# Four graph layers on one core: the last layer's attention rebuilt on stacked hi and lo fp32r pairs, shifts from norms, sums over 63 coordinates

## The chip, the cores and the metric

The kernel runs on one core of one Trainium2 chip. The metric is the device time of one execution in microseconds (us), smaller being better. A run is of state "fast" when it lies within 1.5% of the fastest of its kernel; a kernel that was run only once has state "unknown" and is called a single look here.

## The reference, cut to what matters

Eight batches of 2048 nodes with 64 features pass four graph layers over one adjacency matrix; each is followed by a residual layer norm. The change touches the last one:

```python
def _gat_layer(h, mask, b):
    scores = jnp.einsum('...nd,...md->...nm', h, h)
    scores = jnp.where(mask, scores, NEG)
    attn = jax.nn.softmax(scores, axis=-1)
    return jnp.einsum('...nm,...md->...nd', attn, h) + b
# B, N, C, H, D = 8, 2048, 64, 4, 64
mask = graph + jnp.eye(N, dtype=graph.dtype) > 0
h = jnp.einsum('bnc,hdc->bhnd', x, Wh)                     # four heads
out_h = _gat_layer(h, mask[None, None], bh[None, :, None, :])
cat = jnp.transpose(out_h, (0, 2, 1, 3)).reshape(B, N, H * D)
z = jax.nn.leaky_relu(cat, negative_slope=0.2)
h2 = jnp.einsum('bnk,dk->bnd', z, Wo)
out2 = _gat_layer(h2, mask[None], bo)                      # the "fifth" attention
z2 = jax.nn.leaky_relu(out2, negative_slope=0.2)
# then a layer norm with gamma and beta, + x, and a layer norm without
```

So there are 8 x 5 = 40 attentions, each with a 2048 x 2048 matrix of scores. All is fp32, and the scores go through an exponential, so they need nearly full fp32 accuracy. The input x of the layer is already layer-normed: its 64 features sum to zero, so 63 of them determine the last.

## The kernel before

One attention in layer 3 has two parts. `prepare` makes the projections and finds each row's maximum, in bf16, with a matrix product and a mask product for each tile of 128 x 512 scores. `attend` computes the scores again in fp32, transposed (source node on the partitions), takes the exponential and multiplies the weights by [h | 1].

```python
# prepare: the row maxima
for it in range(NT):                       # NT = 16 tiles of 128 rows
    for c in range(NCH):                   # NCH = 4 chunks of 512 columns
        pa = ps_a.tile([P, CW], F32, name="pa")
        nc.tensor.matmul(pa, hb[:, it * P:(it + 1) * P], hb[:, cs], start=True, stop=False)
        nc.tensor.matmul(pa, neg_id_bf, M[:, it, cs], start=False, stop=True)
        nc.vector.tensor_reduce(mx[:, it, c:c + 1], pa, AX.X, ALU.max)
# ... minus the maxima become the 65th row of the moving side hm ...

# attend: scores, weights, sums
for jt in range(NT):
    pscore = ps_s.tile([P, CW], F32, name="pscore")
    nc.tensor.matmul(pscore, neg_id_bf, MT[:, jt, cs], start=True, stop=False)
    nc.tensor.matmul(pscore, hs[:, jt * P:(jt + 1) * P], hm[:, cs], start=False, stop=True)
    w = wk.tile([P, CW], F32, name="w", bufs=3)
    nc.scalar.activation(w, pscore, AF.Exp)
    nc.tensor.matmul(po, hones[:, jt, hp, hk:hk + 2, :]..., w, start=(jt == 0), stop=(jt == NT - 1))
# ... reciprocal of the denominators, product, bias, leaky relu, product with Wo ...
```

The mask is a matrix product too: minus 2^100 times the identity, times a 0/1 tile in fp8, added into the same accumulator.

## Time and profile before

| | before |
|---|---|
| time, median of the first three runs | 9961.56 us (9957.68 to 9962.04) |
| TensorE / VectorE / ScalarE / GpSimd busy | 92% / 42% / 19% / 6% |
| layers 0 to 2 end at | about 2050 us |
| layer 3, first score to last sum | 2162 to 9932 us |
| granted TensorE clock, mean | 0.914 |

The list of waits over layer 3 adds who waits for whom. Its columns are the waiting engine and line, the engine and line that released it, the total, the number of waits and the longest:

```profile
...
ACT w L564 <- PE pscore L562: 5867.9, 2560, 75.9
DVE rec L567 <- PE po L565: 2836.9, 159, 30.3
...
DVE mx L542 <- PE pa L541: 1192.1, 1502, 4.8
PEld po L565 <- ACT w L564: 1161.0, 1897, 1.6
```

ScalarE and VectorE wait for TensorE, 5868 us at the exponential alone. The last line is the other way round, a weight load of TensorE that is held for the exponential. Most of this passes beside running products.

```profile
6008.02 0.30 PEld L565 LDWEIGHTS po<-w,hones 128*128 128x128 f32 x2 [0.71 <-ACT w L564]
```

The second of two sums starts only when this load does. Two fp32 sums take 1.871 us from start to start in the median of such stretches of this trace (6008.98 - 6007.11 in the prediction's timeline), and 1.715 in the run fp32_sums below, where nothing holds them. So about 0.155 us per two tiles of 512, or 1280 x 0.155 = 199 us in all, goes into this wait (an estimate from the starts). The idle time of 2.1 us that the page gives ahead of the sums (the group L565 in the prediction) does not show it, as the ends of matmul records are modelled. Apart from that the layer hangs on TensorE.

### The profile page before, as it was taken

What the parts mean: (1) busy time and instruction counts of PE and PEld (TensorE: products, weight loads), DVE (VectorE), ACT (ScalarE), POOL (GpSimd) and SP (SyncE); (2) the same over time, 40 slices, a digit from 0 to 9 for tenths busy, and PEclk for the clock granted to TensorE, in tenths of its full rate; (3) what the DMA queues carried; (4) which work ended last, traced back from release to release, by engine and by line L of the source; (5) the groups of instructions that cost most, each with busy time, mean ns of one, the idle gap of its engine ahead of it and who ended that gap; (6) DMA issues with size and microseconds to landing.
All of it is one profiled execution on the core that took longest, in us unless ns stands there. A gap on an engine that the chain in (4) does not pass through costs nothing. (4 is left out here: it accounts for less than half of the span.)

```text
span 9967.4 us, 62454 instructions
## 1 busy us (share of the span) xinstructions
PE 9215.5 (92%) x24992; PEld 3477.5 (35%) x24992; DVE 4228.1 (42%) x5463; ACT 1870.1 (19%) x3156; POOL 597.4 (6%) x471
## 2 busy tenths in 40 slices
PE   3786698679999999999999999999999999999998
PEld 2332244223333333333333333333333333333332
DVE  6899423454334333433443343334333433243423
ACT  1000200012212221222122212221222122212221
POOL 4100301310000000000000000000000000000000
PEclk6898799869989998999899989997999899989997
DMA  2000000000000000000000000000000000000000
GB/s 86 0 0 1 0 0 1 0 1 0 0 0 3 0 0 0 3 0 0 0 3 0 0 0 3 0 0 0 2 0 0 0 3 0 0 0 3 0 0 2
DMA packets 43381, 29.87 MB, mean 3 GB/s; under 512 B 40977, under 2 KB 41041, under 8 KB 41041
## 3 DMA queue, kind: packets, MB, share of 16 engines
q1 hardware_dynamic: 26448, 21.68, 0.7%
q10 hardware_dynamic: 16640, 4.20, 0.2%
q8 instruction: 195, 3.19, 0.1%
q14 instruction: 98, 0.79, 0.0%
HBM read 21.68 MB, written 4.19 MB: 3 GB/s over the span
## 5 line engine op out<-in xcount | busy, mean ns | idle before, releaser
L565 PE MATMUL po<-w,hones 128*128 128x512 f32 x5120 | 2656.5, 622 | 2.1 <-ACT w L564 2.1
L562 PE MATMUL pscore<-hm,hs 65*128 65x512 f32 x5120 | 2650.8, 598 | 0.0
L564 ACT ACTIVATE w<-pscore 128x512 f32<-128x512 f32 x2560 | 1528.6, 597 | 5867.9 <-PE pscore L562 5867.9
L542 DVE TENSOR_REDUCE mx<-pa 128x1 f32<-128x512 f32 x2560 | 1720.9, 691 | 1220.2 <-PE pa L541 1219.2
L567 DVE RECIPROCAL rec<-po 64x512 f32<-64x512 f32 x160 | 536.6, 3353 | 2864.2 <-PE po L565 2864.2
L565 PEld LDWEIGHTS po<-w,hones 128*128 128x128 f32 x5120 | 880.2, 191 | 1245.8 <-ACT w L564 1161.0
L562 PEld LDWEIGHTS pscore<-hm,hs 65*128 65x128 f32 x5120 | 984.7, 193 | 758.1 <-issue 630.7
L540 PE MATMUL pa<-hb 64*128 64x512 bf16 x2560 | 1119.5, 437 | 33.7 <-DVE hb L533 17.2
L541 PE MATMUL pa<-M,neg_id_bf 128*128 128x512 fp8e4 x2560 | 1126.7, 440 | 0.0
L561 PE MATMUL pscore<-MT,neg_id_bf 128*128 128x512 fp8e4 x2560 | 974.8, 382 | 0.2 <-ACT M L458 0.2
L540 PEld LDWEIGHTS <-hb 64*128 64x128 bf16 x2560 | 242.4, 95 | 1299.2 <-issue 1281.3
L270 PE MATMUL acc<-w,H 128*128 128x512 f32 x1024 | 489.1, 632 | 54.0 <-DVE w L267 53.2
L541 PEld LDWEIGHTS <-neg_id_bf 128*128 128x128 bf16 x2560 | 249.6, 97 | 738.6 <-issue 738.6
L534 POOL COPY hm<-hs 64x512 f32<-64x512 f32 x160 | 110.3, 691 | 6234.9 <-ACT hs L532 6234.9
L368 PE MATMUL pa<-R,A 128*128 128x512 f32 x1024 | 453.4, 599 | 9.7 <-POOL R L359 9.3
L561 PEld LDWEIGHTS <-neg_id_bf 128*128 128x128 bf16 x2560 | 249.1, 97 | 474.3 <-issue 469.1
L270 PEld LDWEIGHTS acc<-w,H 128*128 128x128 f32 x1024 | 198.7, 201 | 339.3 <-issue 204.3
L267 DVE SCALAR_TENSOR_TENSOR w<-MT,w 128x1024 f32<-128x1024 fp8e4 x256 | 302.1, 1215 | 0.4
L160 POOL TENSOR_TENSOR ln_rstd<-ln_var,mhalf 128x16 f32<-128x16 f32 (+1 forms) x21 | 151.0, 7189 | 2450.2 <-DVE ln_var L157 2450.2
L368 PEld LDWEIGHTS pa<-R,A 128*128 128x128 f32 x1024 | 191.3, 190 | 269.1 <-issue 245.9
L416 PE MATMUL pa<-Y,A 128*128 128x512 f32 x512 | 219.9, 592 | 0.0
L549 DVE COPY hm<-pm 1x512 f32<-1x512 f32 x160 | 109.0, 682 | 248.4 <-PE pm L548 248.4
(184 smaller groups left out, 3891.9 us busy)
## 6 DMA issues: line engine op xcount, KB each, us to landing
at<-in_adj SPq DMA_DIRECT2D x16, 1024.0 KB, 5.2
X<-in_x ACTq DMA_DIRECT2D x16, 256.0 KB, 7.8
out<-O SPq DMA_DIRECT2D x8, 512.0 KB, 3.8
wt<-in_L_gnn_Wh SPq DMA_DIRECT2D x4, 32.0 KB, 4.6
wo<-in_L_gnn_Wo SPq DMA_DIRECT2D x1, 64.0 KB, 6.0
a<-in_L_gnn_a SPq DMA_DIRECT2D x2, 32.0 KB, 2.9
g<-in_L_gnn_ln_gamma SPq DMA_DIRECT2D x2, 32.0 KB, 2.9
b<-in_L_gnn_ln_beta SPq DMA_DIRECT2D x2, 32.0 KB, 3.1
```

What stands on the lines that cost most here:

```text
L267: nc.vector.scalar_tensor_tensor(w, MT[:, jt, ih * HW:(ih + 1) * HW], 0.0, w, op0=ALU.is_equal, op1=ALU.mult)
L270: nc.tensor.matmul(acc[c], H[:, jt, p, k:k + 2, :].rearrange("p a d -> p (a d)"), w[:, c * CW:(c + 1) * CW], start=(jt == 0), stop=False)
L368: nc.tensor.matmul(pof, A[:, jt], R[:, jt, h].rearrange("p a f -> p (a f)"), start=(jt == 0), stop=False)
L416: nc.tensor.matmul(po, A[:, jt], Y[:, jt], start=(jt == 0), stop=(jt == NT - 1))
L540: nc.tensor.matmul(pa, hb[:, it * P:(it + 1) * P], hb[:, cs], start=True, stop=False)
L541: nc.tensor.matmul(pa, neg_id_bf, M[:, it, cs], start=False, stop=True)
L542: nc.vector.tensor_reduce(mx[:, it, c:c + 1], pa, AX.X, ALU.max)
L561: nc.tensor.matmul(pscore, neg_id_bf, MT[:, jt, cs], start=True, stop=False)
L562: nc.tensor.matmul(pscore, hs[:, jt * P:(jt + 1) * P], hm[:, cs], start=False, stop=True)
L564: nc.scalar.activation(w, pscore, AF.Exp)
L565: nc.tensor.matmul(po, hones[:, jt, hp, hk:hk + 2, :].rearrange("p a d -> p (a d)"), w, start=(jt == 0), stop=(jt == NT - 1))
L567: nc.vector.reciprocal(rec, po[(1 - hk) * D:(2 - hk) * D])
```

## The change

The intent is to spend fewer TensorE passes on the same accuracy, and to put part of the work on the engines that wait.

- **Pairs.** A value v is written as hi + lo: hi is v rounded to fp32r (the type of TensorE's reduced fp32 read, which the prediction cites), lo the remainder. A key side becomes one tile of 128 rows, [hi; lo]. One product against [hi; lo] and one against the swapped [lo; hi] give all four terms of the full product, in two passes of all 128 rows.
- **Weights.** After the exponential VectorE copies w into fp32r (hi) and subtracts (lo). Each is one pass against the stacked value side.
- **Shifts from norms.** A softmax may be shifted by anything that keeps the exponential in range. 0.75 |h_i|^2 plus a sixth of the largest |h|^2 replaces the row maxima, so the whole first pass over the scores, and the second orientation of the mask, go.
- **63 coordinates.** A head's sums are taken over 63 coordinates of the input (the 64th follows), and the freed column is the denominator. The head's projection is applied afterwards to the sum. A fifth attention has no such column; VectorE keeps a running sum of its weights.
- Two tiles of 512 are handled as one wide tile of 1024, and the small work of the next attentions is placed between wide tiles.

The core of the diff, cut:

```diff
-            mx = wk.tile([P, NT, NCH], F32, name="mx")
-            for it in range(NT):
-                for c in range(NCH):
-                    ...
-                    nc.tensor.matmul(pa, hb[:, it * P:(it + 1) * P], hb[:, cs], start=True, stop=False)
-                    nc.tensor.matmul(pa, neg_id_bf, M[:, it, cs], start=False, stop=True)
-                    nc.vector.tensor_reduce(mx[:, it, c:c + 1], pa, AX.X, ALU.max)
 ...
-                    nc.tensor.matmul(pscore, hs[:, jt * P:(jt + 1) * P], hm[:, cs], start=False, stop=True)
-                    nc.scalar.activation(w, pscore, AF.Exp)
-                    nc.tensor.matmul(po, hones[...], w, start=(jt == 0), stop=(jt == NT - 1))
+        def scores(b, h, cp, jt):
+            m1, m2 = state["M", b, h, cp]
+            stat = state["HT" if h == HN else "YT", b]
+            pscore = ps_s.tile([P, 2, CW], F32, name="pscore")
+            sides = [(neg_id_bf, MT[:, jt]), (stat[:, jt * P:(jt + 1) * P], m2), (stat[:, jt * P:(jt + 1) * P], m1)]
+            if h == HN:
+                sides.append((sel[:, HN], shift_row(b)))
+            for k, (lhsT, rhs) in enumerate(sides):
+                for c in range(2):
+                    i0 = c * CW if k in (1, 2) else (2 * cp + c) * CW
+                    nc.tensor.matmul(pscore[:, c], lhsT, rhs[:, i0:i0 + CW], start=(k == 0), stop=(k == len(sides) - 1))
+            w = wk.tile([P, 2 * CW], F32, name="w")
+            nc.scalar.activation(w, pscore.rearrange("p a n -> p (a n)"), AF.Exp)
+            hi = ww.tile([P, 2 * CW], F32R, name="hi")
+            nc.vector.tensor_copy(hi, w)
+            lo = ww.tile([P, 2 * CW], F32R, name="lo")
+            nc.vector.tensor_tensor(lo, w, hi.bitcast(F32), ALU.subtract)
+            if h == HN:
+                ... running sum: nc.vector.tensor_tensor(acc, acc, w, ALU.add)
+        def sums(b, h, cp, jt, hi, lo):
+            stat = state["H2" if h == HN else "Y", b][:, jt]
+            for k, w in enumerate((hi, lo)):
+                for c in range(2):
+                    nc.tensor.matmul(po[c], stat, w[:, c * CW:(c + 1) * CW], start=..., stop=...)
```

## The prediction

> **What bounds the kernel now.** I first read the page's engine rows and slices. TensorE is busy 92% of the span, VectorE 42%, ScalarE 19%, and from the eighth slice on TensorE shows 9 or 8 in every slice: layer 3, the part that is rebuilt, is about four fifths of the time. Then the costliest groups:
>
> ```profile
> PE 9215.5 (92%) x24992; PEld 3477.5 (35%) x24992; DVE 4228.1 (42%) x5463; ACT 1870.1 (19%) x3156; POOL 597.4 (6%) x471
> ...
> L565 PE MATMUL po<-w,hones 128*128 128x512 f32 x5120 | 2656.5, 622 | 2.1 <-ACT w L564 2.1
> L562 PE MATMUL pscore<-hm,hs 65*128 65x512 f32 x5120 | 2650.8, 598 | 0.0
> ...
> L542 DVE TENSOR_REDUCE mx<-pa 128x1 f32<-128x512 f32 x2560 | 1720.9, 691 | 1220.2 <-PE pa L541 1219.2
> ...
> L540 PE MATMUL pa<-hb 64*128 64x512 bf16 x2560 | 1119.5, 437 | 33.7 <-DVE hb L533 17.2
> L541 PE MATMUL pa<-M,neg_id_bf 128*128 128x512 fp8e4 x2560 | 1126.7, 440 | 0.0
> L561 PE MATMUL pscore<-MT,neg_id_bf 128*128 128x512 fp8e4 x2560 | 974.8, 382 | 0.2 <-ACT M L458 0.2
> ```
>
> The counts tell the work: 5120 records for 2560 fp32 products, so an fp32 product of 512 columns is two instructions. The mean durations are those of overlapping instructions; the price is the distance between starts, which I read from the timeline of one steady stretch:
>
> ```profile
> 6004.95 0.38 PE L561 MATMUL pscore<-MT,neg_id_bf 128*128 128x512 fp8e4 x1
> 6004.96 0.41 PEld L562 LDWEIGHTS pscore<-hm,hs 65*128 65x128 f32 x2 [0.33 <-issue]
> 6005.17 1.02 PE L562 MATMUL pscore<-hm,hs 65*128 65x512 f32 x2
> ...
> 6006.03 0.38 PE L561 MATMUL pscore<-MT,neg_id_bf 128*128 128x512 fp8e4 x1
> ...
> 6007.11 2.03 PE L565 MATMUL po<-w,hones 128*128 128x512 f32 x4
> ...
> 6008.98 0.38 PE L561 MATMUL pscore<-MT,neg_id_bf 128*128 128x512 fp8e4 x1
> ```
>
> A mask product takes 6005.17 - 6004.95 = 0.215 us, an fp32 score product 6006.03 - 6005.17 = 0.86, two fp32 sums 6008.98 - 6007.11 = 1.87. Two tiles of 512 take 4.03 us. There the granted clock is 1.00 and TensorE has no gap: layer 3's attention is bound by TensorE's columns, and VectorE waits (1219 us on L541). The row maxima cost more of the same engine: neighbouring starts of L540 and L541 stand 0.32 us apart. Eight times, where the fifth attention's maxima have nothing beside them, the clock falls as well (0.75 between 5800 and 6000 us).
>
> The first score starts at 2162.3 and the last sum at 9931.5: 7769 us, or 194 per attention. Of these, 64 tiles x 2.01 = 129 are scores and sums, 64 x 2 x 0.32 = 41 the maxima, and about 24 projections, transposes and waits. Ahead lie 2051 us for layers 0 to 2 (the last normalisation of X ends at 2050.4) and 111 of preparation; behind, a tail of 36.
>
> **What the Trainium skill says.** "FP8 and Floating Point Precision", TensorE Precision Notes: true fp32 takes four passes through the array, and there is a reduced fp32 read at about 22 bits. The trace agrees on the four: 0.86 is four times 0.215. It does not show the reduced form; I take fp32r as one pass of 0.2135 us, an estimate and the main one. "TensorE: Matmul & The Clock Gate", Back-to-back issue gap, gives N/2.4 + 2.5 ns, thus 216 ns for 512 columns: the mask's 0.215 agrees. "VectorE: DVE Perf Modes", section "Mode 2×_2P", lets a copy within SBUF, but not an operation on two tensors, make two elements per cycle in fp32. The trace agrees: a cast of 512 elements (L533) takes 0.41 us, a tensor_tensor of 512 (L152) 0.69. I assume that a copy into fp32r is such a copy.
>
> **The change, part by part.** All 2560 maxima with their two products, the second mask and most projections go. A key side is now one pair [hi; lo] on 128 rows; two passes, against [hi; lo] and the swapped [lo; hi], give a full product. The weights are split into hi and lo, each one pass against [h hi | h lo]. Counted from the built programs' instruction lists, TensorE in layer 3 at full clock:
> - masks 2560 x 0.215 = 550 us; scores 5120 x 0.2135 = 1093; sums 5120 x 0.2135 = 1093; shifts of the fifth attentions 512 x 0.215 = 110. Together 2846.
> - Small work: sides (256 + 128) x 0.2135 = 82; norms 128 of 256 columns, 14; 64 fp32 products with Wo x 0.86 = 55; 768 transposes x 0.12 (eight L171 in a row span 1.04 us) = 92; about 770 small fp32 products at 0.23 (L518: 0.11 per instruction, two each) = 175. Together 418.
>
> Total 3264, or per batch 408: four head attentions of 74.7 (32 wide tiles x 2.138 + sides 2.6 + output products 3.7), a fifth of 89.6, preparation 20.
>
> VectorE gets new work on each of the 1280 wide tiles (1024 columns): copy to hi, then lo = w - hi, and in the fifth attention a running sum. The copy I put at 0.69 us: a two-per-cycle tensor_scalar of 512 (L421) takes 0.43, to which 512 more, at two per cycle of that page's 0.96 GHz, add 0.27. A two-tensor pass of 1024 costs 1.145 (L267: starts 1.14 apart). lo waits for hi, 0.04. A head tile is thus 1.875, a fifth's tile 0.62 + 1.145 + 1.145 = 2.91. Per head attention: 32 x 1.875 = 60, lo halves of the sides 4 x 0.65, outputs 4 x 1.05, together 67. Per fifth: 93 + outputs 4 + norms 10, together 107.6. Preparation per batch 22. VectorE total: 8 x (4 x 67 + 107.6 + 22) = 3180.
>
> So the two engines end within 3% of each other, and the limit alternates: TensorE in head attentions (74.7 against 67), VectorE in fifths (107.6 against 89.6). Sum of the larger: 32 x 74.7 + 8 x 107.6 + 8 x 20 = 3411 us. ScalarE is far off: 1280 exponentials of at most 1.2 us (twice the 0.597 for 512) and 200 of other work, below 1750.
>
> Coupling: with 90% load on the other engine, and small products in TensorE's fixed order that wait for a copy just before them, some time is lost. The scores run two tiles ahead, which hides about 4.3 us of exp, hi and lo (1.2 + 0.69 + 1.2 = 3.1 at most). I add 6% for queues, such waits and short falls of the clock: 3616.
>
> Start: X spills to HBM and comes back (8 x 512 KB; stores of that size land in 3.8 us today), about 35 us, then Y, norms, shifts and the first side, about 30: first score at 2051 + 65 = 2116, and no second mask is built. Tail about 38. Sum: 2116 + 3616 + 38 = 5770.
>
> **The rivals.**
> 1. The copy into fp32r runs at one element per cycle, as two-tensor work does: 1.145 for 0.69, plus 0.455 x 1280 = 582 on VectorE, which becomes the bound nearly everywhere: 3762 plus a few per cent, end near 6050. For it: no fp32r is in this trace; against it: the cast to bf16 does run fast.
> 2. Weight loads show. Each fp32r pass loads 128 x 128 weights, ten per wide tile, and L540/L541 pay 0.32 - 0.215 = 0.105 for theirs. If eight fp32r passes per tile did so: 1280 x 8 x 0.105 = 1075 more, end near 6800. Against it: between full-array products (L416, a load of 0.19 in each instruction of 0.427, no gap) and before the 65-row L562 loads are hidden; the 64-row shape of L540 looks to be what exposes them, and the change has none in the loop.
> 3. fp32r costs as much as fp32: eight passes of 0.86 per tile, end near 9500. The whole rebuild would be pointless; under 2%.
> 4. The two engines couple worse: VectorE's bursts (building Y, the layer norms) empty the two-tile lead, TensorE idles long enough for the clock to fall. For it: the clock of 0.75 in today's gaps. 12% instead of 6% is 200 us, end near 5980.
>
> All are far below 9962; only the third comes near it.
>
> **Range and chances.** Centre 5770, with a tail upward from rivals 1 and 4; below, if coupling is nearly free, 5560. I say 5800, with 5550 to 6350. Faster by over 2%: 0.985; within 2%: 0.01; slower: 0.005.
>
> **What would show it right or wrong.** In the changed profile: fp32r products one record each, starts 0.21 to 0.22 us apart; 1280 hi copies with a mean near 0.69 (1.2 would be rival 1); lo near 1.22; head attentions of 75 to 80 us with VectorE around 90% busy, fifths of 108 to 115 with TensorE waiting for VectorE; the first score near 2116; granted clock in layer 3 of at least 0.95. Starts 0.3 apart would be rival 2. An attention of 90 us with no engine above 90% would be rival 4.

## The result

The changed kernel takes 5760.24 us in the median (5759.82 to 5765.12, four runs) against 9961.80 us (9957.68 to 9989.94, four runs) of the kernel before in the same rounds. The ratio is 0.5787, 95% interval 0.5774 to 0.5801. Ratios and intervals here are those of fast runs of the same rounds; they are not quite the ratio of the medians (0.5782 here). The result is correct. The prediction was 5800 with a range of 5550 to 6350.

The page of the changed kernel (engine rows; then VectorE's busy tenths in 40 slices; then the costliest groups, with line, engine, operation, tiles, shapes and count, then busy us and mean ns of one, then the idle time just before and its releaser):

```profile
PE 4968.2 (86%) x19861; PEld 3124.3 (54%) x19976; DVE 4396.1 (76%) x5456; ACT 1811.3 (31%) x2156; POOL 555.4 (10%) x344
...
DVE  7499998522233568888888888889889889888897
...
L762 ACT ACTIVATE w<-pscore 128x1024 f32<-128x1024 f32 x1280 | 1313.1, 1026 | 1791.8 <-PE pscore L760 1192.6
L766 DVE TENSOR_TENSOR lo<-w,hi 128x1024 fp32r<-128x1024 f32 x1280 | 1573.9, 1230 | 69.2 <-PE pscore L760 2.3
L760 PE MATMUL pscore<-M,YT 128*128 128x512 f32 x4096 | 1322.7, 443 | 2.7 <-DMA M<-M 2.7
L764 DVE CAST hi<-w 128x1024 fp32r<-128x1024 f32 x1280 | 894.3, 699 | 315.9 <-ACT w L762 313.4
...
L783 PE MATMUL po<-hi,Y 128*128 128x512 f32 x2048 | 668.4, 405 | 30.8 <-DVE hi L764 30.8
L783 PE MATMUL po<-lo,Y 128*128 128x512 f32 x2048 | 662.3, 404 | 30.3 <-DVE lo L766 30.1
```

Three things stand against the page of before. VectorE has gone from 42% to 76%, with 8 or 9 tenths in every slice of layer 3 but the first and the last: it is now nearly as loaded as TensorE. The fp32r products are one record each (4096 score passes for the 32 head attentions: 32 x 32 wide tiles x 4), where an fp32 product of before was two. And ahead of the sums TensorE sits idle 30.8 us for hi and 30.3 for lo: it now sometimes waits for VectorE. The groups print fp32r operands of TensorE as f32.

The step of the loop is read from a steady stretch of TensorE's timeline (start, duration, engine, line, operation, count; equal neighbours are put together):

```profile
3402.93 0.63 PE L783 MATMUL po<-lo,Y 128*128 128x512 f32 x2
3403.40 0.61 PE L760 MATMUL pscore<-MT,neg_id_bf 128*128 128x512 fp8e4 x2
3403.65 1.27 PE L760 MATMUL pscore<-M,YT 128*128 128x512 f32 x4
3404.76 0.63 PE L783 MATMUL po<-hi,Y 128*128 128x512 f32 x2
3405.23 0.63 PE L783 MATMUL po<-lo,Y 128*128 128x512 f32 x2
3405.70 0.39 PE L760 MATMUL pscore<-MT,neg_id_bf 128*128 128x512 fp8e4 x1
```

A wide tile takes 3405.70 - 3403.40 = 2.30 us for ten passes, 0.230 each. The prediction had 0.2135 for eight and 0.215 for two, 2.138 together. Two tiles of 512, the same work, took 4.03 us before, and the maxima came on top. (The first fp32r record after a mask pass stands only 0.03 us behind it, and the next one 0.42 later. I read distances over several passes for that reason.)

To see what each kind of attention costs, I took the distance from its first exponential to the next attention's first exponential, and asked for the busy time of every engine in these windows (window and length in us; busy us and number of instructions of TensorE, weight loads, VectorE, ScalarE and GpSimd; granted clock; DMA share and GB/s):

```profile
2715.20:2794.90 79.70, 79.56 (x363) 57.85 (x364) 67.52 (x81) 37.10 (x40) 0.00 (x0) 1.00 0.06 14
2794.90:2885.60 90.70, 90.19 (x438) 66.44 (x439) 76.03 (x101) 44.89 (x55) 0.00 (x0) 1.00 0.05 12
2885.60:2976.10 90.50, 90.34 (x418) 62.79 (x419) 72.60 (x94) 44.74 (x54) 0.00 (x0) 1.00 0.10 24
2976.10:3072.30 96.20, 95.70 (x439) 62.70 (x443) 93.39 (x109) 36.04 (x38) 3.25 (x2) 1.00 0.03 6
3072.30:3169.90 97.60, 86.39 (x372) 59.70 (x375) 81.33 (x105) 39.40 (x44) 19.02 (x9) 0.95 0.09 22
...
5601.50:5719.40 117.90, 100.97 (x428) 63.66 (x434) 106.05 (x129) 37.16 (x40) 22.57 (x11) 0.91 0.02 5
2105.70:5724.60 3618.90, 3523.35 (x16071) 2467.58 (x16185) 3103.36 (x3830) 1605.04 (x1810) 159.39 (x79) 0.99 0.06 15
```

In order: a plain head attention (79.7 us, TensorE without a gap); one in whose shadow the next batch is prepared (90.7); one that carries the second steps of the batch before (90.5); a fifth attention (96.2, TensorE and VectorE both nearly full); the head attention after a fifth (97.6, where neither is full and the clock falls to 0.95); and, the sixth line, the last fifth. Over the loop, the last line, the clock is 0.99.

Apart from the last fifth, only the attention after a fifth has much time in it in which neither TensorE nor VectorE is full. It is the one in which GpSimd works most (19.0 us; 3.3 in a fifth, none in the other windows above). VectorE's timeline in such a stretch, with the wait ahead of an instruction in brackets:

```profile
2639.79 0.69 DVE L764 CAST hi<-w 128x1024 fp32r<-128x1024 f32 x1
2643.27 1.29 DVE L163 TENSOR_TENSOR O<-O,ln_rstd 128x512 f32<-128x512 f32 x2 [2.79 <-POOL ln_rstd L161]
2644.49 2.29 DVE L766 TENSOR_TENSOR lo<-w,hi 128x1024 fp32r<-128x1024 f32 x1
2646.69 1.76 DVE L764 CAST hi<-w 128x1024 fp32r<-128x1024 f32 x1
...
2654.28 1.28 DVE L151 TENSOR_REDUCE ln_mu<-O 128x8 f32<-128x512 f32 x2 [3.62 <-POOL O L713]
```

and GpSimd's in the same stretch:

```profile
2639.96 3.28 POOL L161 TENSOR_TENSOR ln_rstd<-ln_var,mhalf 128x16 f32<-128x16 f32 x1 [8.27 <-DVE ln_var L158]
...
2645.76 2.14 POOL L166 TENSOR_TENSOR O<-O,b 128x512 f32<-128x512 f32 x1
...
2651.88 2.36 POOL L713 TENSOR_TENSOR O<-O,x 128x1024 f32<-128x1024 f32 x1
```

L163 needs GpSimd's power (3.28 us), and the lo and hi of the attention that is running come behind it in VectorE's program. While VectorE waits, TensorE runs out of hi and lo tiles. Besides, a copy to hi takes 1.76 us instead of 0.69 and a subtraction to lo 2.29 instead of 1.22 where GpSimd is at work. The Trainium skill, "SBUF — State Buffer", Who interferes with whom, says that a VectorE instruction in a two-port mode, or with two SBUF inputs, and a GpSimd instruction that reads SBUF exclude each other for the whole instruction. The trace of these lines agrees: GpSimd's L166 ends at 2645.76 + 2.14 = 2647.90, and the copy, recorded from 2646.69, ends at 2648.45, 0.55 us later, near the 0.69 that it takes alone (GpSimd's spans are rough).

### The profile page after: what moved, and what is told of

Same layout as the page of the kernel before. It is cut to its first block, busy times and chain, and to the rows that moved or that the text cites. A ratio compares the mean times of both kernels' runs of the same rounds, so it can differ in the third digit from the quotient of the medians.

```text
span 5763.3 us, 51217 instructions
## 1 busy us (share of the span) xinstructions
PE 4968.2 (86%) x19861; PEld 3124.3 (54%) x19976; DVE 4396.1 (76%) x5456; ACT 1811.3 (31%) x2156; POOL 555.4 (10%) x344
## 4 chain that ended last, share of the span: by engine, by line
PE 63%; issue 7%; DVE 6%; POOL 5%; ACT 0%; SPq 0%; DMA 0%; another core or an unknown queue 0%; POOLq 0%; DVEq 0%; ACTq 0%
PE pscore L760 29%; PE po L783 19%; PE pa L369 8%; POOL ln_rstd L161 2%; PE pm L633 2%; DVE lo L766 2%; DVE hi L764 1%; PE pm L664 1%; PE pm L614 1%; PE pa L371 1%; POOL O L166 1%; PE pm L546 1%; PE pm L656 1%; POOL O L165 0%; DVE ln_mu L151 0%
## 5 line engine op out<-in xcount | busy, mean ns | idle before, releaser
L762 ACT ACTIVATE w<-pscore 128x1024 f32<-128x1024 f32 x1280 | 1313.1, 1026 | 1791.8 <-PE pscore L760 1192.6
L766 DVE TENSOR_TENSOR lo<-w,hi 128x1024 fp32r<-128x1024 f32 x1280 | 1573.9, 1230 | 69.2 <-PE pscore L760 2.3
L760 PE MATMUL pscore<-M,YT 128*128 128x512 f32 x4096 | 1322.7, 443 | 2.7 <-DMA M<-M 2.7
L764 DVE CAST hi<-w 128x1024 fp32r<-128x1024 f32 x1280 | 894.3, 699 | 315.9 <-ACT w L762 313.4
L760 PEld LDWEIGHTS pscore<-M,YT 128*128 128x128 f32 x4096 | 778.0, 191 | 236.2 <-issue 12.2
L783 PE MATMUL po<-hi,Y 128*128 128x512 f32 x2048 | 668.4, 405 | 30.8 <-DVE hi L764 30.8
L783 PE MATMUL po<-lo,Y 128*128 128x512 f32 x2048 | 662.3, 404 | 30.3 <-DVE lo L766 30.1
L783 PEld LDWEIGHTS po<-lo,Y 128*128 128x128 f32 x2048 | 385.6, 191 | 131.9 <-DVE lo L766 44.2
L783 PEld LDWEIGHTS po<-hi,Y 128*128 128x128 f32 x2048 | 385.0, 189 | 127.5 <-DVE hi L764 41.8
L760 PEld LDWEIGHTS <-neg_id_bf 128*128 128x128 bf16 x2560 | 180.2, 102 | 310.9 <-issue 295.4
```

What stands on the lines that cost most here:

```text
L760: nc.tensor.matmul(pscore[:, c], lhsT, rhs[:, i0:i0 + CW], start=(k == 0), stop=(k == len(sides) - 1))
L762: nc.scalar.activation(w, pscore.rearrange("p a n -> p (a n)"), AF.Exp)
L764: nc.vector.tensor_copy(hi, w)
L766: nc.vector.tensor_tensor(lo, w, hi.bitcast(F32), ALU.subtract)
L783: nc.tensor.matmul(po[c], stat, w[:, c * CW:(c + 1) * CW], start=(jt == 0 and k == 0), stop=(jt == NT - 1 and k == 1))
```

## The experiments

### What each half of the change is worth

**The kernel before with the norm shifts alone.** The maxima, and with them the second mask, go; the scores and sums stay as before.

```diff
-            for it in range(NT):
-                for c in range(NCH):
-                    nc.tensor.matmul(pa, hb[...], hb[:, cs], ...); nc.tensor.matmul(pa, neg_id_bf, M[:, it, cs], ...)
-                    nc.vector.tensor_reduce(mx[:, it, c:c + 1], pa, AX.X, ALU.max)
-            nc.vector.tensor_reduce(m, mx, AX.X, ALU.max)
+            sq = wk.tile([P, NT, D], F32, name="sqn", bufs=1)
+            nc.scalar.activation(sq, hones[:, :, hp, 2 * hk], AF.Square)
+            nc.vector.tensor_reduce(m, sq, AX.X, ALU.add)
+            ... the largest of all nodes, by two transposes, to every partition as ms (a sixth of it)
+            nc.vector.tensor_scalar(m, m, 0.75, ms, op0=ALU.mult, op1=ALU.add)
```

> The kernel before with one part of the change alone: the shifts come from squared norms (0.75 of a row's own plus a sixth of the largest), so all 2560 maxima, their mask and the second mask go; the fp32 products stay. Theory: the maxima's two products cost what the starts in the trace of before add up to, 0.64 us per tile warm and 1.08 cold, about a quarter of them cold: 2560 x 0.74 = 1890 us, and the second mask about 40, less about 1 us per attention for the norms: about 8050 us, ratio 0.81. The rest of the gain, 2290 us, then belongs to the fp32r pairs. Rival: the maxima ran in the shadow of waits of the attention's own chain (exp, then sums): then much less goes, 8500 or more.

Measured: 8174.01 us (8171.67 to 8175.95), correct, ratio 0.8203 (0.8189 to 0.8217). The 1789 us less are 42.6% of the change's gain, 1789 of 9963.1 - 5760.2 = 4203. The first theory was nearer than the rival; its 8050 was 124 us too low.

**The change without hi and lo of the weights.** The sums take w as it is, in fp32, against the same stacked side.

```diff
-            hi = ww.tile([P, 2 * CW], F32R, name="hi")
-            nc.vector.tensor_copy(hi, w)
-            lo = ww.tile([P, 2 * CW], F32R, name="lo")
-            nc.vector.tensor_tensor(lo, w, hi.bitcast(F32), ALU.subtract)
...
-            for k, w in enumerate((hi, lo)):
-                for c in range(2):
-                    nc.tensor.matmul(po[c], stat, w[:, c * CW:(c + 1) * CW], ...)
+            for c in range(2):
+                nc.tensor.matmul(po[c], stat.bitcast(F32), hi[:, c * CW:(c + 1) * CW], ...)   # hi is w here
```

> The changed kernel with one part undone: the weights are not split into hi and lo, the sums are fp32 products of four passes against the same stacked value side. TensorE gets 2 x 0.86 us instead of 4 x 0.231 per wide tile, VectorE loses the copy and the subtraction (1.9 us). Theory: TensorE's columns bind, so +0.80 x 1280 = 1020 us, less what is lost today to VectorE (about 150): 6600 to 6800. Rival: VectorE's split work slows the loop by about what the passes save: below 6100.

Measured: 6651.50 us (6646.61 to 6655.67), correct, ratio 0.6675 (0.6665 to 0.6685). The window of a plain head attention of this kernel, columns as above:

```profile
2873.60:2978.00 104.40, 104.26 (x363) 59.81 (x364) 6.90 (x16) 37.14 (x40) 0.00 (x0) 1.00 0.04 11
```

VectorE is busy 6.9 us of 104.4: the split of the weights moves 61 us of work onto an idle engine (6.9 to 67.5) and takes 25 us off the bound one (104.4 to 79.7). In the whole it is worth 6651.5 - 5760.2 = 891 us. The remaining 8174.0 - 6651.5 = 1523 us lie between the two kernels: scores in pairs, the 63 coordinates, the wide tiles and the new placement. The scores are most of that: 2560 x (0.86 - 2 x 0.230) = 1024 us, an estimate from the starts in the two traces. About 199 us are the wait of the sums for the exponential, which the kernel before has and this one has not:

```profile
2900.94 1.88 PE L778 MATMUL po<-w,Y 128*128 128x512 f32 x4
2902.65 0.59 PE L760 MATMUL pscore<-MT,neg_id_bf 128*128 128x512 fp8e4 x2
```

Two fp32 sums take 2902.65 - 2900.94 = 1.71 us here; in before_norm they take 1.87, as in the kernel before. The other 300 I did not take apart.

### What sets 0.230 us

Neighbouring passes with the same weights go to different accumulator banks, and each has its own weight load. Either could add the 16 ns.

**Another order of banks.** The loop over the two halves goes outside.

```diff
-            for k, (lhsT, rhs) in enumerate(sides):
-                for c in range(2):
+            for c in range(2):
+                for k, (lhsT, rhs) in enumerate(sides):
 ...
-            for k, w in enumerate((hi, lo)):
-                for c in range(2):
+            for c in range(2):
+                for k, w in enumerate((hi, lo)):
```

> The same passes in another order: all passes into one PSUM bank in a row, then those into the other, instead of alternating. It asks why a pass took 0.231 us and not the 0.2135 of the prediction. Theory A (every pass pays about 12 ns for following one into another bank; in the kernel before a mask product took 0.226 after a change of bank and 0.216 without): bank changes per wide tile fall from 10 to 4, so a tile falls from 2.30 to about 2.23, a plain head attention from 79.7 to about 77.4, and the kernel by 80 to 100 us to about 5670. Theory B (an fp32r pass waits for its own weight load, 0.188 + 0.042 = 0.230 us, which starts only when the pass before it starts): the fp32r passes stay at 0.230, the time stays within 20 us of 5760.

It was sent together with the unchanged kernel, which measures what a repetition is worth:

> The changed kernel once more, as the anchor for the runs beside it. All theories: 5760 us within 0.3%, a plain head attention (the third of a batch) of 79.7 us at 79.5 us of TensorE, fp32r starts 0.231 us apart.

Measured: the repetition 5762.56 us (5760.36 to 5770.34), correct, ratio 0.5785 (0.5775 to 0.5794), so it repeats to 0.05%. The other order 5789.35 us (5785.07 to 5793.64), correct, ratio 0.5810 (0.5802 to 0.5819); a plain head attention 80.2 us instead of 79.7. Fewer changes of bank do not make a pass shorter; theory A is out. The order is a little slower. In the starts, a mask pass comes 0.238 us after an fp32r pass, and this order has twice as many such changes. That these are the 27 us is argued, not shown.

**The sums in bf16.** hi, lo and the value side become bf16, which halves the bytes of the stationary side, and of the moving side too, and leaves the number of passes.

```diff
+                nc.scalar.copy(Yb, Y.bitcast(F32))                  # and H2b for the fifth attentions
-            hi = ww.tile([P, 2 * CW], F32R, name="hi")
+            hi = ww.tile([P, 2 * CW], BF16, name="hi")
-            lo = ww.tile([P, 2 * CW], F32R, name="lo")
+            lo = ww.tile([P, 2 * CW], BF16, name="lo")
-            stat = state["H2" if h == HN else "Y", b][:, jt]
+            stat = state["H2b" if h == HN else "Yb", b][:, jt]
```

> The weights' halves and the value sides in bf16 instead of fp32r in the sums alone, order of banks as in the changed kernel; less exact on purpose, so the result may miss the tolerance. A bf16 weight load takes 0.097 us instead of 0.188. Theory A (bank changes): sum passes 0.226 to 0.228 us, a tile 2.28. Theory B (weight loads): sum passes 0.215, a tile 2.24, a plain head attention 77.7 us.

Measured: 5710.86 us, a single look, correct. The sums' timeline in a steady stretch:

```profile
3300.26 0.60 PE L789 MATMUL po<-hi,Yb 128*128 128x512 bf16 x2
3300.70 0.59 PE L789 MATMUL po<-lo,Yb 128*128 128x512 bf16 x2
3301.14 0.59 PE L766 MATMUL pscore<-MT,neg_id_bf 128*128 128x512 fp8e4 x2
```

The lo passes take (3301.14 - 3300.70) / 2 = 0.22, singly 0.215 to 0.216, and the score passes, left in fp32r, still take about 0.23. A plain head attention falls from 79.7 to 77.8 us, the number that theory B had given. The load records are 98 ns long instead of 188 to 190. The Trainium skill, "TensorE: Matmul & The Clock Gate", Weight-path perf modes, says that the fast weight load is on for 128 weights in a type other than FP32; the trace agrees as far as it goes, with 98 ns for bf16 and 190 for both fp32 and fp32r.

That looks like a proof of theory B, which I had read from single records: nearly each load starts 2 to 3 ns after the product ahead of it has started, lasts 188 to 190 ns, and its own product starts about 40 ns after it ends, 0.188 + 0.042 = 0.230. But the trace of the changed kernel holds a case that contradicts it. The norms are fp32r products of 256 columns, four in a row, each with a full weight load of its own:

```profile
2857.57 0.62 PE L783 MATMUL po<-lo,Y 128*128 128x512 f32 x2
2858.03 0.64 PE L595 MATMUL pm<-Vr,YT 128*128 128x256 f32 x4
2858.51 0.61 PE L760 MATMUL pscore<-MT,neg_id_bf 128*128 128x512 fp8e4 x2
```

```profile
2857.80 0.66 PEld L595 LDWEIGHTS pm<-Vr,YT 128*128 128x128 f32 x4
```

They take (2858.51 - 2858.03) / 4 = 0.12 us each, and the records of their loads are 188 ns long as well. Loads overlap each other, and a product starts before the record of its load has ended. So the length of the load doesn't set 0.230: theory B had the number right and its mechanism is not what the trace shows. What stands is that the time goes with the type. Against half of a mask pass's 0.215, an fp32r pass of 256 columns takes about 0.012 us more; against a whole one, an fp32r pass of 512 takes 0.015 more; with both sides in bf16 nothing is left, but for the first bf16 pass behind an fp32r one (0.226). It isn't four-byte operands by themselves either, since an fp32 product of before, two instructions 0.43 apart, comes to 0.215 per pass. Which of the two sides in fp32r adds the time, and why, stays open: this run changed both.

### What holds the fifth attentions

**No running sum.** The sum of a fifth's weights is left out and a constant takes its place, so the result is wrong (relative error 0.354).

```diff
-                    nc.vector.tensor_copy(state["acc", b, cp], w)
+                    nc.vector.memset(state["acc", b, cp], 1.0)
...
-                    nc.vector.tensor_tensor(acc, acc, w, ALU.add)
+                    pass
```

> The running sum of the weights in the fifth attentions is left out (it is set to one), the result is wrong on purpose. It asks what bounds the fifth attentions, where both engines read 97% to 99% busy. Theory: VectorE (hi + sum + lo = 3.0 us a tile, 32 of them 96.2, just what is measured): without the sum TensorE's 12 passes bind, a fifth falls from 96.25 to 88 to 91 us, and the kernel by about 50 to 70 us. Rival: TensorE binds (95.75 of 96.25 busy): a fifth stays above 95 us.

Measured: 5742.39 us, a single look. A fifth attention:

```profile
2980.30:3074.10 93.80, 93.32 (x430) 62.27 (x436) 68.09 (x84) 36.54 (x39) 1.48 (x2) 1.00 0.03 6
```

VectorE loses 25 us and the fifth 2.4, from 96.2 to 93.8. It lies between the two expectations: VectorE did set the end of a fifth, but TensorE was only 2.4 us behind, since its shift passes and its 0.230 count there too. The last fifth, with nothing after it, fell from 117.9 to 105.2. The whole kernel gained 18 to 20 us, not the 50 to 70 of the theory: besides the small step of the fifths, the attentions after a fifth grew by about 1.2 us each.

### What holds the attention after a fifth

**The layer norm in pieces.** The two layer norms of an output stood in one block in VectorE's queue; here they are cut into four pieces that stand several wide tiles apart. GpSimd keeps its share.

```diff
-                layer_norm([O[:, 0:B], O[:, B:NT]], wk, g3, b3)
-                nc.gpsimd.tensor_tensor(O, O, x_of(b), ALU.add)
-                layer_norm([O[:, 0:B], O[:, B:NT]], wk)
-                nc.sync.dma_start(out[b]..., O)
+                s1, m1 = norm_parts([O[:, 0:B], O[:, B:NT]], wk, g3, b3)
+                s2, m2 = norm_parts([O[:, 0:B], O[:, B:NT]], wk)
+                ...
+                slow.extend([s1] + pause * 3 + [rest] + pause * 7 + [s2] + pause * 4 + [last])
```

> The closing layer norms of a batch are cut into four pieces that are emitted several tiles apart, with the same instructions. Theory: the 18 us by which the second attention of a batch (97.6) exceeds a plain one (79.7) is VectorE standing in its fixed order on GpSimd (pow, gamma, beta, +x: 78 us of VectorE waits in all), so six attentions fall to 80 to 86 us and the kernel by 60 to 110 us, to 5650 to 5700. Rival: it is VectorE's amount of work (10 us of norms per batch beside GpSimd that slows VectorE): then at most 30 us are won, 5730 or more.

Measured: 5732.93 us (5730.35 to 5739.55), correct, ratio 0.5755 (0.5746 to 0.5763). 30 us less, at the limit that I had set for the rival; the attention after a fifth takes 93.1 to 94.7 us instead of 97.6, not the 80 to 86 of the theory. But the edit did not take the order out of the queue. In the attention after the second fifth VectorE waits for the power as long as before, first in the changed kernel, then here:

```profile
DVE O L163 <- POOL ln_rstd L161: 5.6, 2, 2.8
```

```profile
DVE O L181 <- POOL ln_rstd L176: 5.6, 2, 2.8
```

In all VectorE waits 6.8 us for GpSimd there (9.8 in the changed kernel), and its copies and subtractions take 5.0 us longer than alone (3.5 before). The longest copy to hi now takes 2.86 us: the pieces still meet GpSimd.

**GpSimd's share to VectorE.** In addition, gamma, beta, the bias and the residual go from GpSimd to VectorE; only the power stays.

```diff
-                nc.gpsimd.tensor_tensor(v, v, over(gamma, shape), ALU.mult)
-                nc.gpsimd.tensor_tensor(v, v, over(beta, shape), ALU.add)
+                eng = nc.vector if len(shape) == 3 and len(chunks) == 2 else nc.gpsimd
+                eng.tensor_tensor(v, v, over(gamma, shape), ALU.mult)
+                eng.tensor_tensor(v, v, over(beta, shape), ALU.add)
...
-                nc.gpsimd.tensor_tensor(o, o, over(bo, o.shape), ALU.add)
+                nc.vector.tensor_tensor(o, o, over(bo, o.shape), ALU.add)
...
-                    nc.gpsimd.tensor_tensor(O, O, xb, ALU.add)
+                    nc.vector.tensor_tensor(O, O, xb, ALU.add)
```

> The spread layer norms, with the work that GpSimd did on the output (gamma, beta, both additions) given to VectorE; only the pow stays on GpSimd. The run before left the second attention of a batch at 93 to 95 us. Theory: what remains is GpSimd's work stretching VectorE's (the hi copy took 1.77 us beside it, 0.69 alone) and VectorE waiting for it: with 5 us more of VectorE's own work but none beside GpSimd, a second attention falls to 88 to 91 us, the kernel to 5695 to 5720. Rival: VectorE's amount decides: the 5 us come on top, 5735 to 5770.

Measured: 5679.10 us (5677.73 to 5681.24), correct, ratio 0.5700 (0.5691 to 0.5708), better than I had expected. The attention after a fifth:

```profile
3060.40:3146.10 85.70, 82.10 (x373) 57.86 (x375) 80.19 (x112) 39.33 (x45) 7.50 (x2) 1.00 0.10 25
```

85.7 us instead of 97.6, at full clock, with VectorE busy 80.2 us, about what it was before (81.3). VectorE has more instructions and no more busy time: with GpSimd at rest (7.5 us, the power alone) the copies take 0.69 and the subtractions 1.22 again. VectorE no longer waits for GpSimd here, not even for the power (once in the whole loop, 2.8 us), as other work now stands between the power and its use. So of the 83 us that the two steps gain, the pieces brought 30, and the end of the waits (6.8 us per attention) and of the stretched copies and subtractions (5.0 us) together 54. How the 54 split between the two is not shown; no run has one without the other.

### A version that beats both

**The layer norms as just shown, and the sums in bf16.**

> The kernel with all layer-norm steps but the power on VectorE in four spread pieces (5679 us), and in addition hi, lo and the value sides of the sums in bf16. If each part of the gain is what its own run showed and they do not overlap, the bf16 weights take another 50 us, near 5628. But the attention after a fifth now has VectorE busy 80 of 86 us, and a fifth is held by VectorE at about 96 us once TensorE's passes are cheaper, so only the 24 other head attentions can gain their 1.9 us each: 5633. Both say 5620 to 5645. Rival: the two parts get in each other's way (VectorE's lead shrinks where its norms now lie), and the time stays above 5655. Plain head attention 77.5 to 78, fifth 95 to 96.

The edit is the two diffs above together. Measured: 5621.17 us (5617.97 to 5627.31), correct, ratio 0.5648 (0.5641 to 0.5656). The two parts add up: 58 us less than with the layer norms alone. (This run and the next were made on another chip, in whose rounds the kernel before was some 7 us faster; by the ratios it is 52.) A plain head attention takes 77.8 us, the one after a fifth 84.3, a fifth 95.3 with VectorE busy 94.0 of it.

**And the cross pass in bf16, and a fifth's hi on ScalarE.** Of the two score passes, the one against the swapped side carries only the mixed terms, of the size of lo, so that I expected little harm from rounding its sides to bf16; the result is still correct. And as VectorE holds the fifths, ScalarE, at a third of its time, takes their copy to hi. To make room for the bf16 copies, the fp32 value sides, which are needed only while they are built, have one buffer instead of three (not in this cut).

```diff
-            nc.vector.tensor_copy(hi, w)
+            (nc.scalar.copy if h == HN else nc.vector.tensor_copy)(hi, w)
...
-            m2 = wy.tile([P, 2 * CW], F32R, name="M2")
-            nc.sync.dma_start(m2[0:D].bitcast(F32), m1[D:P].bitcast(F32))
-            nc.sync.dma_start(m2[D:P].bitcast(F32), m1[0:D].bitcast(F32))
+            mb = wy.tile([P, 2 * CW], BF16, name="Mb")
+            nc.scalar.copy(mb, m1.bitcast(F32))
+            m2 = wy.tile([P, 2 * CW], BF16, name="M2")
+            nc.sync.dma_start(m2[0:D], mb[D:P])
+            nc.sync.dma_start(m2[D:P], mb[0:D])
...
-            sides = [(neg_id_bf, MT[:, jt]), (stat[:, jt * P:(jt + 1) * P], m2), ...
+            sides = [(neg_id_bf, MT[:, jt]), (statb[:, jt * P:(jt + 1) * P], m2), ...
```

> As the run before, and two more: the cross pass of the scores (swapped side against its own bf16 copy of the stationary side) in bf16, and in the fifth attentions the copy to hi on ScalarE in place of VectorE. Theory: the two cross passes of a wide tile fall from 0.230 to 0.216 us, 0.9 us per attention; in a fifth VectorE loses 32 copies of 0.69, falls from 93 to about 72 us, and TensorE (about 90 us) binds instead of VectorE, so fifths come to 91 to 93. That is 24 x 0.9 + 8 x 3.5 = 50 us less: 5575 to 5600, plain head near 77. Rival: the exponential and the copy share ScalarE's one queue, 2.1 us per tile of 2.9, and the two-tile lead no longer hides exp, hi and lo in a row; then fifths stay at 96 or grow and the time stays at 5610 or above.

Measured: 5550.38 us (5547.51 to 5556.76, five runs), correct, ratio 0.5579 (0.5571 to 0.5586). A plain head attention, a fifth, and the attention after it:

```profile
2681.20:2758.00 76.80, 76.80 (x366) 39.99 (x365) 67.47 (x81) 38.90 (x43) 0.00 (x0) 1.00 0.03 8
2935.20:3025.80 90.60, 90.60 (x437) 46.89 (x436) 80.97 (x84) 70.09 (x72) 0.00 (x0) 1.00 0.02 4
3025.80:3109.50 83.70, 81.35 (x382) 42.22 (x380) 76.75 (x107) 40.46 (x45) 7.42 (x2) 0.98 0.08 20
```

The fifth has come down from 95.3 to 90.6, and TensorE has no gap left in it; the rival, a ScalarE queue too long for the lead, is out. In all, the eight fifths gave 44 us (789 to 745) and the heads 25. I had expected 28 and 22; the difference is mostly the last fifth, 109.7 to 95.2. VectorE's time in a fifth fell by 13 us, and with the attention after it by 16 (173.8 to 157.8), where 32 copies of 0.69 are 22. The rest is in the way of counting: records of neighbouring VectorE instructions overlap a little. Their durations in the two windows sum to 189.1 and 167.8 us, 21 less, and the overlap falls from 14.9 to 9.6. This version is 210 us, 3.6%, faster than the changed kernel.

## Why the prediction was right

The time was within 40 us, 0.7%, and close to the working sum of 5770. The loop, 3616 predicted, ran from the first score at 2103.7 to the last sum at 5724.6, 3621. But not every term held, and the agreement of the sum owes something to errors that cancel.

- **One pass for fp32r (rival 3 out): right in kind, mis-sized.** The estimate of 0.2135 us, called the main one, measured 0.230. What adds the 16 ns is not known; it goes with fp32r and not with the length of the weight load, so it is not rival 2 (which had feared 105) in a small form either. A plain head attention came to 79.7 us instead of 74.7: eight passes x 32 tiles x 0.0165 = 4.2, and the mask passes, 0.228 instead of 0.215, 0.8 more. Over 32 heads it is 160 us.
- **The copy at two elements per cycle (rival 1 out): right.** 0.699 us mean, 0.69 predicted; lo 1.230 against 1.22 predicted. VectorE's 67 us in a head attention were 67.5, and its 3180 in the whole loop 3103.
- **Fifths bound by VectorE at 107.6: wrong in size and place.** The work was there, 93.4 us in the fifth and 81.3 - 67.5 = 13.8 more in the attention after it, 107.2 together. But outputs and layer norms fall into the next attention, where VectorE had room. In the fifth itself the two engines end almost together, as the run without the running sum shows. With preparation and second steps I had 861 + 160 = 1021 us; the trace has 805.5 for the eight fifths, and 148 by which the attentions with preparation and second steps exceed plain ones, 953 together. That is 68 too much in the prediction.
- **6% for coupling, 205 us: about twice too much.** I had put it down to queues, waits of small products and short falls of the clock, spread over everything. In plain heads there was none of it; TensorE has no gap. What there was lies in one place, the six head attentions that follow a fifth (all eight second heads of a batch, these six among them, take 747.5 us, eight plain ones 637.5): 110 us, the bursts of the layer norm that rival 4 named, plus what I had not thought of, GpSimd's hold on VectorE's copies. The two layer-norm runs got 83 us back, 73 of them in these six; the other 37 of the 110 remained. So rival 4's mechanism was real, but its amount, 12% or some 410 us, was not: 110 is 3% of 3411.

The account in one line, over the sum of 3411 before coupling: + 160 (passes) - 68 (fifths and preparation) + 110 (attentions after a fifth) = + 202, where I had added 205. That these agree is luck: the passes, which I had thought right, filled what the coupling left over.

- **Start and tail: right.** First score at 2103.7 instead of 2116, tail 38.7 instead of 38.
- **Clock of at least 0.95: right.** 0.99 over the loop; 0.93 to 0.95 in the attentions after a fifth, in which TensorE idles, and 0.91 in the last fifth.
- **Signs to look for.** "Fifths of 108 to 115 with TensorE waiting for VectorE" was not seen, except for the last two (110.1 and 117.9), which carry more than their own work. "Starts 0.21 to 0.22 apart" was missed by a little, and bf16 on both sides brought it about. The sign of rival 4, an attention of 90 us with no engine above 90%, was there: 97.6 us after each fifth, with TensorE at 89% and VectorE at 83%.
- **Slips in the working.** The fp32 sums of before were read as 0.94 us each with TensorE full; 0.08 of it is the wait for the exponential. Rival 3's end near 9500 is about the loop alone: TensorE's 3264 + 1280 x 8 x (0.86 - 0.2135) = 9884, with start and tail about 12,040, which is above the 9962 of before and not just below. And 93 + 4 + 10 for a fifth are 107, not 107.6. None of the three moves the 5800.

The gain itself, 4203 us, splits by the runs into 1789 for the row maxima, 1523 for scores in pairs with the rest of the rebuilding, and 891 for the split of the weights. Each part was measured at one place in this order; in another order the parts could differ.

## What to carry to other kernels

When one engine is full and another idle, a matrix product in fp32 can be bought with cheaper passes and elementwise work: here 61 us of VectorE per attention paid for 25 us of TensorE. Once two engines are both near full, look at the stretches where neither is full. Here a queue in strict order and a third engine that kept VectorE waiting or slowed it were at work, and moving work off the third engine was faster even though the second got more to do. Idle time in a page can miss a wait of TensorE; compare the distances between starts with the same products elsewhere. And before a theory with the right sum is believed, look in the trace for a case in which it would give another number: the 256-column products were there all along.

## What the Trainium skill lacked or had wrong

- "TensorE: Matmul & The Clock Gate", LDWEIGHTS: it gives columns / 1.2 ns, so 107 for 128 columns, and this section makes no difference between types (the one on the fast weight load does). The records here are 98 ns long for bf16 and 188 to 190 for fp32 and fp32r. It also lacks what a load costs in a stream: fp32r products of 256 columns, each with a load record of 188 ns, follow each other at 0.12 us.
- The same page, Back-to-back issue gap: it puts a sustained stream at 131 ns per product of 512 columns and calls the 216 of its formula that of a single one. In the steady streams here no distance over several products is below 0.215 to 0.216 us each; none comes near 131. (A single fp32r record can stand 28 ns behind a mask pass; the two passes then take 0.447 together.)
- "FP8 and Floating Point Precision", TensorE Precision Notes: it names the reduced read of fp32 but gives no rate. The runs show one record and 0.230 us for 512 columns of it (0.12 for 256), against 0.86 for four passes of fp32. No page that I used says what a change from an fp32r pass to a bf16 one costs: 0.238 us from start to start and 0.226 to 0.228 to the next one, against 0.230 between two fp32r passes and 0.216 between two bf16 ones.
- "SBUF — State Buffer", Who interferes with whom, is confirmed, and worth a number for planning: beside GpSimd's layer-norm steps the fp32r copy of 1024 elements took 1.76 us instead of 0.69 and the subtraction 2.29 instead of 1.22; taking GpSimd's elementwise steps away was worth 54 us, with the waits for GpSimd that went with them.
